# Two-layer graph and state-space kernel: one product for step sizes, gate, B and C, six residual buffers, another order of the scan's small products

## The chip, the cores and the metric

The kernel runs on one core of a Trainium2 chip. A core has five engines that work side by side, each through its own queue in order: TensorE (PE, matrix products, with its weight loads shown apart as PEld), VectorE (DVE), ScalarE (ACT, activations), GpSimd (POOL) and SyncE (SP, which issues transfers). The metric is the device time of the whole kernel in microseconds (us), the median of several runs. All data are float32 unless a line says otherwise.

## What is computed

x is (32, 512, 256), adj is (32, 512, 512) of zeros and ones. Two layers follow each other; each adds a graph part and a feed-forward part to x. Layer 0 is a graph sum with a tropical and a gated classical feed-forward. Layer 1, which the change touches, is an attention over adj (`_L1_gnn_ref`) and a mixer (`_L1_ffn_ref`). The mixer, for each of 32 batches, gathers 512 tokens into 64 slices with softmax weights sw, runs a state-space scan in both directions over the slices, and spreads the result back:

```python
fx = (x @ W_fx.T + b_fx)...                 # 8 heads of 64
sw = softmax((xm @ W_slice.T + b_slice) / temp)
st = einsum('bhnc,bhng->bhgc', fx, sw) / (sw.sum(2) + 1e-5)
ot = _hydra(st, ...)
out = einsum('bhgc,bhng->bhnc', ot, sw) @ out_w.T + out_b

def _hydra(u, ...):
    zxbcdt = u @ in_w.T                     # z 512 | x 512, B 64, C 64 | dt 16
    dt = softplus(concat(dt[:, :, :8], flip(dt[:, :, 8:])) + dt_bias)
    xBC = silu(causal conv of width 3 over xBC + conv_b)
    # h = h * exp(dt * -exp(A_log)) + dt B x ;  y = h C, forward and backward
    y = y_fw + y_bw (each shifted by one) + x * (x @ fcD_w.T + D)
    y = y * silu(z)
    return rms_norm(y) @ out_w.T
```

The kernel does not step through the recurrence: with 64 slices it writes the scan as one product with a decay matrix (the file's gp, segp, decay, mix, yp below).

## The kernel before, in words

`layer1_plain` (L863 on) builds layer 1. Batches are taken in groups of two (GB = 2), so 16 groups. A mixer group is `mixer(g)`: `slices` of each of its two batches, `tokens`, `scan`, and `unslice` of each batch. Two slices of 64 fill the 128 partitions, so a tile in the scan has both batches of its group.

Beside the mixer runs the attention of later batches, `attentions()`: for batch b the products avp and adp (L1258, L1263) are woven with `prepare(b+1)`, which gathers the batch's rows of x, builds its mask, and makes the per-head products hp (L1188). The mixer yields a number at points in its course; the number times PACE is added to a credit, and for each whole unit of credit one step of attention is emitted there. A batch can be prepared only when its rows of x have a buffer: x has AHEAD_X = 2·GB + 1 = 5 buffers (L895), a buffer is free when the batch five before it has been stored by `unslice`. The order of the instructions of each engine is fixed when the kernel is built.

The steps, by tile names:

- `slices`: normalisation of the batch (statistics std, shiftd, x4 by ACT at L1141; the same for the attention with stc, shiftc, hv), lgp (logits, L1344), sw (Exp by ACT L1345, then softmax work on DVE, L1346 to L1351), yTp (L1356) and the turned swT.
- `tokens`: uTp (L1375), rnp (L1381) and on DVE uT.
- `scan`: xp (L1409), which ACT copies to xpad; bcp (L1418), copied to bpad; dtp (L1437 and L1402), from which DVE makes sp, the step sizes (softplus, with ACT's Exp at L1446 and Ln at L1452); zp (L1402), to which ACT applies Silu for z; convolutions with DVE (conv, L1426 to L1428) and Silu with ACT (L1464 for xT, L1471 for B and C, cpad being C with a zero at each end). Then seg (DVE, L1490), gp (L1496), segp (L1500), decay (ACT Exp, L1502), xtp, qp, dq, gm, mix and back (DVE, L1514 to L1519), yp (L1526), y, yTp, oTp (L1544), msp and rms (L1552, L1555), vp (L1566).
- `unslice`: outp (L1576), the addition to the residual rows of x (DVE, L1578), and the store.

psum tiles of this code have four rotating buffers. The weights inT hold the columns in the order z, x, B and C, dt. Each product of float32 shows as two matmuls in the profile.

Of the kernel before, what the change touches and what calls it, by code (L numbers as in the profile page):

```python
# [8 lines left out]
F32 = mybir.dt.float32  # L9
# [4 lines left out]
AF = mybir.ActivationFunctionType  # L14
ALU = mybir.AluOpType
# [4 lines left out]
P = 128  # L20
# [4 lines left out]
LN_EPS = 1e-5  # L25
# [839 lines left out]
def layer1_plain(tc, ident, eps, x2s, ranks, adj, w, out, over, ps):  # L865
# [3 lines left out]
    nc = tc.nc  # L869
    B = adj.shape[0]  # L870
    SEG = B // len(x2s)
    GB = 2
# [19 lines left out]
    AHEAD = 3  # L892
    ATT = 2 * (AHEAD + 2) + AP + 1
    HW = P // AH
    AHEAD_X = 2 * GB + 1  # L895
    PACE = 1.04 * GB * (TURNS + STEPS) / WANTED

    SMALL = 30.0 * 30.0 / D
# [2 lines left out]
    with ExitStack() as ctx:  # L901
# [23 lines left out]
        with tc.tile_pool(name="raw0", bufs=1, side="right") as raw:  # L925
            prod = raw.tile([P, DC, AH, HO], F32, tag="prod", name="prod")
            norm2 = raw.tile([P, DC, 2, AH], F32, tag="norm2", name="norm2")
            for i, name in enumerate(("a_dst", "a_src")):
                dst = wa[:, :, AH * (HO + i) : AH * (HO + i + 1)]
# [30 lines left out]
        bc_w = const("bc_w", [S, 2, KW], w["hy_conv_w"][DI:].rearrange("(c p) k -> p c k", p=S))  # L960
        bc_b = const("bc_b", [S, 2], w["hy_conv_b"][DI:].rearrange("(c p) -> p c", p=S))
        skip = const("skip", [P, H], w["hy_D"].partition_broadcast(P))
        dtb = ctile("dtb", [P, 4, H])
        for i in range(4):
            nc.sync.dma_start(dtb[:, i, :], w["hy_dt_bias"].partition_broadcast(P))
        nega = const("nega", [P, H], w["hy_A_log"].partition_broadcast(P))
        nc.scalar.activation(nega, nega, AF.Exp)
# [20 lines left out]
        wfxT = ctile("wfxT", [P, DC, DI])  # L988
# [3 lines left out]
        inT = ctile("inT", [P, KC, DIN])  # L992
        hoT = ctile("hoT", [P, KC, DI])
        owT = ctile("owT", [P, KC, D])
        fcT = ctile("fcT", [P, KC, H])

        with tc.tile_pool(name="raw", bufs=2, side="right") as raw:
# [4 lines left out]
            for i in range(2):  # L1002
# [4 lines left out]
            nc.sync.dma_start(bs, w["b_slice"].rearrange("(o n) -> o n", o=1))  # L1007


            pieces = [(dst, w[name], r0)  # L1010
                      for dst, name in ((wfxT, "W_fx"), (inT, "hy_in_w"), (hoT, "hy_out_w"), (owT, "out_w"),
                                        (fcT, "hy_fcD_w"))
                      for r0 in range(0, w[name].shape[0], P)]

            def fetch(i):

# [27 lines left out]
            for c in range(DC + 1):  # L1044
                M = P if c < DC else 1
                for i in range(H // KC):

                    half = slice(i * C, (i + 1) * C)
                    px = psum("mm", f"wslp{c}_{i}")
# [3 lines left out]
                    px = px[:M, : KC * G].rearrange("p (k g) -> p k g", k=KC)  # L1053
# [3 lines left out]
                    else:  # L1057
                        dst = bsl[:, i :: H // KC, :]
# [60 lines left out]
        sb = ctx.enter_context(tc.tile_pool(name="s1", bufs=2, reuse_waits="tile"))  # L1119
# [272 lines left out]
        def scan(g, uT):  # L1392


            T = GB * G
# [4 lines left out]
            def tok_matmul(p, c0, n):  # L1400
                for c in range(KC):
                    nc.tensor.matmul(p, uT[:, c, :], inT[:, c, c0 : c0 + n], start=c == 0, stop=c == KC - 1)  # L1402
# [3 lines left out]
            px = psum("any", f"xp{g}")  # L1406
            for k in range(KC):
                for c in range(KC):
                    nc.tensor.matmul(px[:, k * T : (k + 1) * T], inT[:, c, DI + k * P : DI + (k + 1) * P],  # L1409
                                     uT[:, c, :], start=c == 0, stop=c == KC - 1)  # L1410
            xpad = sb.tile([P, KC, GB, LP], F32, tag="xpad", name=f"xpad{g}", bufs=1)
            nc.gpsimd.memset(xpad[:, :, :, : KW - 1], 0.0)
            nc.scalar.copy(xpad[:, :, :, KW - 1 :], px.rearrange("p (k j l) -> p k j l", k=KC, j=GB))
            pb = psum("any", f"bcp{g}")
            for i in range(2):
                c0 = 2 * DI + i * S
                for c in range(KC):
                    nc.tensor.matmul(pb[:S, i * T : (i + 1) * T], inT[:, c, c0 : c0 + S], uT[:, c, :],  # L1418
                                     start=c == 0, stop=c == KC - 1)
            bpad = sb.tile([S, 2, GB, LP], F32, tag="bpad", name=f"bpad{g}", bufs=1)  # L1420
            nc.gpsimd.memset(bpad[:, :, :, : KW - 1], 0.0)
            nc.scalar.copy(bpad[:, :, :, KW - 1 :],
                           pb[:S, : 2 * T].rearrange("p (k j l) -> p k j l", k=2, j=GB))

            def conv(src, wts, dst):
                nc.vector.tensor_scalar_mul(dst, src[:, :, 0:G], wts[:, 0:1])  # L1426
                for q in range(1, KW):
                    nc.vector.scalar_tensor_tensor(dst, src[:, :, q : q + G], wts[:, q : q + 1], dst,  # L1428
                                                   ALU.mult, ALU.add)

            pd = psum("any", f"dtp{g}")
            for j in range(GB):
                for i in range(2):
                    for c in range(KC):
                        nc.tensor.matmul(pd[i * G : (i + 1) * G, j * H : (j + 1) * H],  # L1437
                                         uT[:, c, j * G : (j + 1) * G],
                                         inT[:, c, DT0 + i * H : DT0 + (i + 1) * H],
                                         start=c == 0, stop=c == KC - 1)  # L1440
            tok_matmul(pd[:, 2 * H : 4 * H], DT0, 2 * H)
            sp = sb.tile([P, 5, 4 * H], F32, tag="sp", name=f"sp{g}")
            v, e, u, r, dt = (sp[:, i, :] for i in range(5))
            nc.vector.tensor_add(v, pd[:, : 4 * H], dtb.rearrange("p i h -> p (i h)"))
            nc.vector.scalar_tensor_tensor(e, v, -1.0, v, ALU.mult, ALU.min)
            nc.scalar.activation(e, e, AF.Exp)  # L1446

# [5 lines left out]
            nc.vector.tensor_sub(u, u, e)  # L1453
            nc.vector.scalar_tensor_tensor(dt, v, 0.0, u, ALU.max, ALU.add)

            pz = psum("any", f"zp{g}")
            tok_matmul(pz, 0, DI)
            z = sb.tile([P, DI], F32, tag="z", name=f"z{g}", bufs=1)
            nc.scalar.activation(z, pz, AF.Silu)
            xT = inner(f"xT{g}")  # L1460
            for k in range(KC):
                dst = chunks(xT)[:, k, :]
                conv(xpad[:, k], conv_w[:, k, :], dst.rearrange("p (j l) -> p j l", j=GB))
                nc.scalar.activation(dst, dst, AF.Silu, bias=conv_b[:, k : k + 1])  # L1464
            bcT = sb.tile([S, 2, GB, G], F32, tag="bcT", name=f"bcT{g}", bufs=1)
            cpad = sb.tile([S, GB, G + 2], F32, tag="cpad", name=f"cpad{g}", bufs=1)
            nc.gpsimd.memset(cpad[:, :, 0 : G + 2 : G + 1], 0.0)
            for i in range(2):
                conv(bpad[:, i], bc_w[:, i, :], bcT[:, i])
                dst = bcT[:, 0] if i == 0 else cpad[:, :, 1 : G + 1]  # L1470
                nc.scalar.activation(dst, bcT[:, i], AF.Silu, bias=bc_b[:, i : i + 1])  # L1471

            la = sb.tile([P, GB, H], F32, tag="la", name=f"la{g}")
# [15 lines left out]
            yield 7  # L1491

            pg = psum("any", f"gp{g}")
            for j in range(GB):
                for i in range(2):
                    nc.tensor.matmul(pg[j * G : (j + 1) * G, i * G : (i + 1) * G], bcT[:, 0, j, :],  # L1496
                                     cpad[:, j, 2 * i : 2 * i + G], start=True, stop=True)
            pl = psum("any", f"segp{g}")
            for j in range(GB):
                nc.tensor.matmul(pl[j * G : (j + 1) * G, :], seg_l, seg[j], start=True, stop=True)  # L1500
            decay = inner(f"decay{g}")
            nc.scalar.activation(decay, pl, AF.Exp)  # L1502
# [17 lines left out]

            yield 7
            py = psum("any", f"yp{g}")
            for j in range(GB):
                half = slice(j * G, (j + 1) * G)
                for h in range(H):
                    nc.tensor.matmul(py[half, h * C : (h + 1) * C], heads(mix)[half, h, :],  # L1526
                                     heads(xk)[half, h, :], start=True, stop=True)
            y = inner(f"y{g}")
# [3 lines left out]
            ms = sb.tile([P, 1], F32, tag="ms", name=f"ms{g}")  # L1532
# [13 lines left out]
            oT = inner(f"oT{g}")  # L1546
            nc.scalar.copy(oT, po)

            pm = psum("any", f"msp{g}")
            for j in range(GB):  # L1550
                for i in range(P // C):
                    nc.tensor.matmul(pm[i * G : (i + 1) * G, j : j + 1], ident[:, j * G : (j + 1) * G], ms,  # L1552
                                     start=True, stop=True)
            rms = sb.tile([P, GB], F32, tag="rms", name=f"rms{g}")
            nc.vector.tensor_scalar(rms, pm[:, :GB], 1.0 / DI, LN_EPS, ALU.mult, ALU.add)  # L1555
            nc.gpsimd.tensor_tensor(rms, rms, eps[:, 1:2].to_broadcast([P, GB]), ALU.pow)
            yield 2

# [690 lines left out]
```

## Time and profile before

| what | us |
|---|---|
| time, median of 3 runs | 4320.41 (4319.69 to 4325.92) |
| the profiled execution's own time | 4319.15 |
| its span | 4317.4 |
| TensorE busy in the span | 3852.3 |
| VectorE busy | 3233.1 |
| ScalarE busy | 2290.3 |
| mixer groups' first xp product, from first to last | 2490.99 to 4249.27 |
| per group, mean of 15 steps | 117.2 |

The kernel's first 2330 us or so are layer 0. The groups of layer 1 have a step of 115 to 120 us, and 103 at the end, where no attention is left to weave in. Group 14 has little of it and group 15 none. Busy time adds all instructions of an engine; the time that an engine waits is shown with what ended the wait. A name such as `xp<-inT,uT` is output tile, then operands; the number after x counts instructions. The granted clock of TensorE is in tenths or as a share, 1.00 being full.

### The profile page before, as it was taken

How to read it: one execution, taken by the hardware profiler on the slowest of the kernel's cores; microseconds unless marked ns; L12 is line 12 of the kernel's file. 1: busy time of each engine (PE TensorE's matmuls, PEld its weight loads, DVE VectorE, ACT ScalarE, POOL GpSimd, SP SyncE). 2: the span in 40 equal slices, each digit the busy share in tenths (PEclk: the TensorE clock that was granted, in tenths of full speed). 3: DMA queues.
4: the chain of work that ended last, by engine and by line, in shares of the span. 5: the costliest groups of instructions: out<-in, count | busy, mean ns of one | idle time of the engine just before them, and what ended most of it. 6: DMA issues, size and time to landing. Idle time of an engine off the chain costs nothing.

```text
span 4317.4 us, 57903 instructions
## 1 busy us (share of the span) xinstructions
PE 3852.3 (89%) x20311; PEld 2446.7 (57%) x20311; DVE 3233.1 (75%) x7008; ACT 2290.3 (53%) x4756; POOL 1540.2 (36%) x1940
## 2 busy tenths in 40 slices
PE   5567998899999999889998899999999999999997
PEld 4454565566655665555555355565555555565555
DVE  6668877888788977877775777767777777778763
ACT  3344655556655656556664455545554455555432
POOL 2355643664435644354332222222222222222210
PEclk8678999999999999999999999999999999999998
DMA  4557654665546654386542322222222232222210
GB/s 130 161 160 228 191 162 133 192 214 168 149 127 218 197 165 136 109 279 192 153 128 69 78 67 71 79 62 67 74 69 69 76 79 76 75 69 74 62 30 16
DMA packets 260811, 524.16 MB, mean 121 GB/s; under 512 B 39800, under 2 KB 131588, under 8 KB 260509
## 3 DMA queue, kind: packets, MB, share of 16 engines
q0 software_dynamic: 124800, 366.28, 29.5%
q1 hardware_dynamic: 135708, 154.08, 11.4%
q8 instruction: 162, 2.65, 0.3%
q14 instruction: 141, 1.15, 0.1%
HBM read 463.11 MB, written 57.17 MB: 121 GB/s over the span
## 4 chain that ended last, share of the span: by engine, by line
PE 35%; DVE 26%; DMA 10%; issue 9%; POOL 8%; ACT 5%; SPq 0%; POOLq 0%; DVEq 0%; ACTq 0%
PE clsp L623 5%; DVE att L1221 4%; PE gatep L623 4%; PE po L652 3%; PE avp L1258 3%; DVE acc L637 3%; DMA rows<-table,xs 2%; PE yTp L1356 2%; DVE best L599 2%; DMA best<-table,xs 2%; DVE sw L1351 2%; DMA rows<-table,tops 2%; DVE sst L1349 2%; DVE sw L1346 2%; PE oTp L1544 1%
## 5 line engine op out<-in xcount | busy, mean ns | idle before, releaser
L623 PE MATMUL clsp<-xnT,wc 128*128 128x512 f32 x1024 | 522.4, 629 | 47.2 <-ACT cls L625 40.3
L623 PE MATMUL gatep<-xnT,wg 128*128 128x512 f32 x1024 | 496.8, 604 | 9.4 <-ACT gate L625 7.4
L652 PE MATMUL po<-wd,acc 128*128 128x256 f32 x2048 | 451.7, 380 | 5.2 <-DVE acc L641 4.3
L652 PEld LDWEIGHTS po<-wd,acc 128*128 128x128 f32 x2048 | 386.8, 190 | 70.7 <-issue 9.1
L1221 DVE SCALAR_TENSOR_TENSOR att<-own,other,mask 128x512 f32<-128x512 f32 x512 | 365.7, 743 | 78.5 <-DMA own<-ownd 78.5
L599 DVE SCALAR_TENSOR_TENSOR best<-rows,xs,best 128x1024 f32<-128x1024 f32 x212 | 271.0, 1280 | 132.6 <-ACT best L593 74.9
L637 DVE SCALAR_TENSOR_TENSOR acc<-past,fld,acc 128x512 f32<-128x512 f32 x448 | 332.1, 744 | 32.5 <-ACT past L636 24.3
L623 PEld LDWEIGHTS gatep<-xnT,wg 128*128 128x128 f32 x1024 | 196.1, 196 | 249.9 <-issue 198.4
L632 ACT ACTIVATE acc<-tz,fld 128x512 f32<-128x512 f32 x256 | 199.0, 777 | 260.1 <-PE tz L630 235.2
L636 ACT ACTIVATE past<-tz,fld 128x512 f32<-128x512 f32 x448 | 291.3, 693 | 73.3 <-DVE acc L637 72.7
L596 POOL DMA_INDIRECT rows<-table,xs x212 | 252.9, 1193 | 188.6 <-DVE best L599 124.8
L623 PEld LDWEIGHTS clsp<-xnT,wc 128*128 128x128 f32 x1024 | 183.7, 200 | 184.6 <-issue 113.3
L435 PE MATMUL pm<-h,adj 128*128 128x258 f32 (+1 forms) x1024 | 182.3, 325 | 98.5 <-DVE keep L428 35.7
L1258 PE MATMUL avp<-att,hv 128*32 128x512 f32 x2048 | 254.9, 603 | 13.9 <-DVE att L1221 13.8
L625 ACT ACTIVATE gate<-gatep,fld 128x512 f32<-128x512 f32 x256 | 175.5, 685 | 158.3 <-PE gatep L623 129.2
L1344 PE MATMUL lgp<-wsl,x4T 128*128 128x512 f32 x512 | 243.0, 613 | 16.6 <-ACT sw L1345 7.2
L1356 PE MATMUL yTp<-sw,x 128*128 128x512 f32 x512 | 237.8, 602 | 18.9 <-DVE sw L1351 18.2
L554 POOL DMA_INDIRECT xs<-rows_of,order x128 | 155.0, 1211 | 266.8 <-DVE acc L637 104.3
L1162 POOL DMA_INDIRECT x<-x2s,ranks x128 | 136.5, 1066 | 297.7 <-DVE att L1221 133.3
L1309 POOL TENSOR_TENSOR mu<-mu,eps 128x16 f32<-128x16 f32 x32 | 111.2, 3475 | 348.1 <-DVE mu L1308 347.9
L1576 PE MATMUL outp<-v,swT 128*128 128x256 f32 x1024 | 227.6, 381 | 0.0
L435 PEld LDWEIGHTS pm<-h,adj 128*128 128x128 f32 x1024 | 152.5, 214 | 123.9 <-issue 73.0
(590 smaller groups left out, 8643.8 us busy)
## 6 DMA issues: line engine op xcount, KB each, us to landing
adj<-in_adj POOLq DMA_DIRECT2D x128, 256.0 KB, 5.6
ai<-in_adj SPq DMA_DIRECT2D x128, 256.0 KB, 2.8
x<-added POOLq DMA_DIRECT2D x64, 512.0 KB, 5.2
own<-ownd SPq DMA_DIRECT2D x128, 256.0 KB, 3.6
rows_of<-keep SPq DMA_DIRECT2D x32, 550.0 KB, 4.3
x<-in_x SPq DMA_DIRECT2D x32, 512.0 KB, 6.6
xs<-bd POOLq DMA_DIRECT2D x32, 512.0 KB, 5.7
x2s<-xs SPq DMA_DIRECT2D x32, 512.0 KB, 3.0
```

Of the source, the lines that this page charges most:

```text
L435: nc.tensor.matmul(pm[:, : c1 - c0], a[:, i, t * P : (t + 1) * P], h[:, i, c0:c1], start=i + c0 == 0, stop=i + 1 == NT and c0 > 0)
L596: nc.gpsimd.indirect_dma_start(out=row, out_offset=None, in_=table, in_offset=bass.IndirectOffsetOnAxis(ap=idxs[:, k : k + 1].bitcast(U32) ...
L599: nc.vector.scalar_tensor_tensor(m, row, vals[:, k : k + 1], m, ALU.add, ALU.max)
L623: nc.tensor.matmul(pf, wf[:, c, f * P : (f + 1) * P], xnT[:, c, :], start=c == 0, stop=c == DC - 1)
L636: nc.scalar.activation(r, z, AF.Relu, bias=fld[:, f, AT + b : AT + b + 1])
L637: nc.vector.scalar_tensor_tensor(y, r, fld[:, f, CH + b : CH + b + 1], y, ALU.mult, ALU.add)
L652: nc.tensor.matmul(po[:, i, :], acc[f][:, t * P : (t + 1) * P], wd[:, f, :], start=f == 0, stop=f == FC - 1)
L1221: nc.vector.scalar_tensor_tensor(e, own[h], other[:, j, h : h + 1], mask[:, j, :], ALU.max, ALU.mult)
L1258: nc.tensor.matmul(pv[p][k * HW : (k + 1) * HW, :], hv[:, j, h, e : e + HW], weighed[b, h, j], **ends)
L1344: nc.tensor.matmul(pf, xnT[:, c, t * P : (t + 1) * P], wsl[:, c, :], start=c == 0, stop=c == DC - 1)
L1356: nc.tensor.matmul(py, xn[:, t, c * P : (c + 1) * P], sw[:, t, :], start=t == 0, stop=t == NT - 1)
L1576: nc.tensor.matmul(po[:, :D], swT[:, k, t * P : (t + 1) * P], v[:, k, :], start=k == 0, stop=k == KC - 1)
```

## The change

The columns of inT are stored in the order dt (16), z (512), x (512), B and C (128). B and C are one product over 128 output rows, into the first 128 columns of the bcp bank; dt and the first half of z are one product of 272 columns into the rest of that bank; the second half of z has its own bank with 256 columns. The products that wrote dt half by half in the partitions of each direction are gone: DVE instead adds the bias with one instruction over the 16 columns and four over halves of the partitions. B and C are convolved as one tile of 128 partitions. z and the convolution and Silu of B and C are written ahead of those of x. The mean square of rms is read on DVE by four small instructions and no longer copied by PE (msp). The loops of gp and yp have the halves of the group innermost, segp runs its halves in reverse. sp and la have one buffer, x has six.

```diff
-    AHEAD_X = 2 * GB + 1
+    AHEAD_X = 2 * GB + 2
...
-        dtb = ctile("dtb", [P, 4, H])
-        for i in range(4):
+        dtb = ctile("dtb", [P, 2, H])
+        for i in range(2):
...
-            pb = psum("any", f"bcp{g}")
-            for i in range(2):
-                c0 = 2 * DI + i * S
-                for c in range(KC):
-                    nc.tensor.matmul(pb[:S, i * T : (i + 1) * T], inT[:, c, c0 : c0 + S], uT[:, c, :],
-                                     start=c == 0, stop=c == KC - 1)
-            bpad = sb.tile([S, 2, GB, LP], F32, tag="bpad", name=f"bpad{g}", bufs=1)
...
+            pb, pz = psum("any", f"bcp{g}"), psum("any", f"zp{g}")
+            for c in range(KC):
+                nc.tensor.matmul(pb[:, :T], inT[:, c, DIN - P :], uT[:, c, :], start=c == 0, stop=c == KC - 1)
+            first = 2 * H + DI // 2
+            tok_matmul(pb[:, T : T + first], 0, first)
+            tok_matmul(pz[:, : DI // 2], first, DI // 2)
+            bpad = sb.tile([P, GB, LP], F32, tag="bpad", name=f"bpad{g}", bufs=1)
+            nc.gpsimd.memset(bpad[:, :, : KW - 1], 0.0)
+            nc.scalar.copy(bpad[:, :, KW - 1 :], pb[:, :T].rearrange("p (j l) -> p j l", j=GB))
...
-            pd = psum("any", f"dtp{g}")
-            for j in range(GB):
-                for i in range(2):
-                    for c in range(KC):
-                        nc.tensor.matmul(pd[i * G : (i + 1) * G, j * H : (j + 1) * H],
-                                         uT[:, c, j * G : (j + 1) * G],
-                                         inT[:, c, DT0 + i * H : DT0 + (i + 1) * H],
-                                         start=c == 0, stop=c == KC - 1)
-            tok_matmul(pd[:, 2 * H : 4 * H], DT0, 2 * H)
-            sp = sb.tile([P, 5, 4 * H], F32, tag="sp", name=f"sp{g}")
+            pd = pb[:, T : T + 2 * H]
+            sp = sb.tile([P, 5, 4 * H], F32, tag="sp", name=f"sp{g}", bufs=1)
             v, e, u, r, dt = (sp[:, i, :] for i in range(5))
-            nc.vector.tensor_add(v, pd[:, : 4 * H], dtb.rearrange("p i h -> p (i h)"))
+            nc.vector.tensor_add(v[:, 2 * H :], pd, dtb.rearrange("p i h -> p (i h)"))
+            for i in range(2):
+                for j in range(GB):
+                    half = slice(j * G, (j + 1) * G)
+                    nc.vector.tensor_add(v[i * G : (i + 1) * G, j * H : (j + 1) * H],
+                                         pd[half, i * H : (i + 1) * H], dtb[half, 0, :])
...
-            pz = psum("any", f"zp{g}")
-            tok_matmul(pz, 0, DI)
             z = sb.tile([P, DI], F32, tag="z", name=f"z{g}", bufs=1)
-            nc.scalar.activation(z, pz, AF.Silu)
+            nc.scalar.activation(z[:, : DI // 2], pb[:, T + 2 * H : T + first], AF.Silu)
+            nc.scalar.activation(z[:, DI // 2 :], pz[:, : DI // 2], AF.Silu)
+            bcT = sb.tile([P, GB, G], F32, tag="bcT", name=f"bcT{g}", bufs=1)
+            cpad = sb.tile([S, GB, G + 2], F32, tag="cpad", name=f"cpad{g}", bufs=1)
+            nc.gpsimd.memset(cpad[:, :, 0 : G + 2 : G + 1], 0.0)
+            conv(bpad, bc_w, bcT)
+            for half, dst in ((slice(0, S), bcT[:S]), (slice(S, P), cpad[:, :, 1 : G + 1])):
+                nc.scalar.activation(dst, bcT[half], AF.Silu, bias=bc_b[half])
...
-            for j in range(GB):
-                for i in range(2):
-                    nc.tensor.matmul(pg[j * G : (j + 1) * G, i * G : (i + 1) * G], bcT[:, 0, j, :],
+            for i in range(2):
+                for j in range(GB):
+                    nc.tensor.matmul(pg[j * G : (j + 1) * G, i * G : (i + 1) * G], bcT[:S, j, :],
                                      cpad[:, j, 2 * i : 2 * i + G], start=True, stop=True)
             pl = psum("any", f"segp{g}")
-            for j in range(GB):
+            for j in reversed(range(GB)):
                 nc.tensor.matmul(pl[j * G : (j + 1) * G, :], seg_l, seg[j], start=True, stop=True)
...
-            for j in range(GB):
-                half = slice(j * G, (j + 1) * G)
-                for h in range(H):
+            for h in range(H):
+                for j in range(GB):
+                    half = slice(j * G, (j + 1) * G)
                     nc.tensor.matmul(py[half, h * C : (h + 1) * C], heads(mix)[half, h, :],
                                      heads(xk)[half, h, :], start=True, stop=True)
...
-            pm = psum("any", f"msp{g}")
+            rms = sb.tile([P, GB], F32, tag="rms", name=f"rms{g}")
             for j in range(GB):
                 for i in range(P // C):
-                    nc.tensor.matmul(pm[i * G : (i + 1) * G, j : j + 1], ident[:, j * G : (j + 1) * G], ms,
-                                     start=True, stop=True)
-            rms = sb.tile([P, GB], F32, tag="rms", name=f"rms{g}")
-            nc.vector.tensor_scalar(rms, pm[:, :GB], 1.0 / DI, LN_EPS, ALU.mult, ALU.add)
+                    nc.vector.tensor_scalar(rms[i * G : (i + 1) * G, j : j + 1], ms[j * G : (j + 1) * G], 1.0 / DI, LN_EPS,
+                                            ALU.mult, ALU.add)
```

The preparation of the weights follows (the pieces of in_w are copied to the new columns, conv weights and biases of B and C lie in 128 partitions).

More of the change, by code (lines that the diff above doesn't have):

```diff
@@ L959, in layer1_plain @@
         conv_b = const("conv_b", [P, KC], w["hy_conv_b"][:DI].rearrange("(c p) -> p c", p=P))
-        bc_w = const("bc_w", [S, 2, KW], w["hy_conv_w"][DI:].rearrange("(c p) k -> p c k", p=S))
-        bc_b = const("bc_b", [S, 2], w["hy_conv_b"][DI:].rearrange("(c p) -> p c", p=S))
+        bc_w = const("bc_w", [P, KW], w["hy_conv_w"][DI:])
+        bc_b = const("bc_b", [P, 1], w["hy_conv_b"][DI:].rearrange("(p o) -> p o", o=1))
         skip = const("skip", [P, H], w["hy_D"].partition_broadcast(P))
-        dtb = ctile("dtb", [P, 4, H])
-        for i in range(4):
+        dtb = ctile("dtb", [P, 2, H])
+        for i in range(2):
             nc.sync.dma_start(dtb[:, i, :], w["hy_dt_bias"].partition_broadcast(P))
@@ L1007, in layer1_plain @@
             nc.sync.dma_start(bs, w["b_slice"].rearrange("(o n) -> o n", o=1))
[L1010 to L1013, printed above, removed]
+            pieces = [(dst, src, r0)
+                      for dst, src in ((wfxT, w["W_fx"]), (inT[:, :, 2 * H :], w["hy_in_w"][:DT0]),
+                                       (inT[:, :, : 2 * H], w["hy_in_w"][DT0:]), (hoT, w["hy_out_w"]),
+                                       (owT, w["out_w"]), (fcT, w["hy_fcD_w"]))
+                      for r0 in range(0, src.shape[0], P)]
             def fetch(i):
@@ L1408, in scan @@
                 for c in range(KC):
-                    nc.tensor.matmul(px[:, k * T : (k + 1) * T], inT[:, c, DI + k * P : DI + (k + 1) * P],
-                                     uT[:, c, :], start=c == 0, stop=c == KC - 1)
+                    x0 = 2 * H + DI + k * P
+                    nc.tensor.matmul(px[:, k * T : (k + 1) * T], inT[:, c, x0 : x0 + P], uT[:, c, :],
+                                     start=c == 0, stop=c == KC - 1)
             xpad = sb.tile([P, KC, GB, LP], F32, tag="xpad", name=f"xpad{g}", bufs=1)
@@ L1413, in scan @@
             nc.scalar.copy(xpad[:, :, :, KW - 1 :], px.rearrange("p (k j l) -> p k j l", k=KC, j=GB))
-            pb = psum("any", f"bcp{g}")
-            for i in range(2):
-                c0 = 2 * DI + i * S
-                for c in range(KC):
-                    nc.tensor.matmul(pb[:S, i * T : (i + 1) * T], inT[:, c, c0 : c0 + S], uT[:, c, :],
-                                     start=c == 0, stop=c == KC - 1)
-            bpad = sb.tile([S, 2, GB, LP], F32, tag="bpad", name=f"bpad{g}", bufs=1)
-            nc.gpsimd.memset(bpad[:, :, :, : KW - 1], 0.0)
-            nc.scalar.copy(bpad[:, :, :, KW - 1 :],
-                           pb[:S, : 2 * T].rearrange("p (k j l) -> p k j l", k=2, j=GB))
+            pb, pz = psum("any", f"bcp{g}"), psum("any", f"zp{g}")
[7 more added lines that the diff above has]
+            nc.scalar.copy(bpad[:, :, KW - 1 :], pb[:, :T].rearrange("p (j l) -> p j l", j=GB))
             def conv(src, wts, dst):
@@ L1464, in scan @@
                 nc.scalar.activation(dst, dst, AF.Silu, bias=conv_b[:, k : k + 1])
-            bcT = sb.tile([S, 2, GB, G], F32, tag="bcT", name=f"bcT{g}", bufs=1)
-            cpad = sb.tile([S, GB, G + 2], F32, tag="cpad", name=f"cpad{g}", bufs=1)
-            nc.gpsimd.memset(cpad[:, :, 0 : G + 2 : G + 1], 0.0)
-            for i in range(2):
[L1469 to L1475, printed above, removed]
+            la = sb.tile([P, GB, H], F32, tag="la", name=f"la{g}", bufs=1)
             nc.vector.tensor_mul(la, dt[:, : GB * H].rearrange("p (j h) -> p j h", j=GB),
@@ L1493, in scan @@
             pg = psum("any", f"gp{g}")
-            for j in range(GB):
-                for i in range(2):
-                    nc.tensor.matmul(pg[j * G : (j + 1) * G, i * G : (i + 1) * G], bcT[:, 0, j, :],
+            for i in range(2):
+                for j in range(GB):
+                    nc.tensor.matmul(pg[j * G : (j + 1) * G, i * G : (i + 1) * G], bcT[:S, j, :],
                                      cpad[:, j, 2 * i : 2 * i + G], start=True, stop=True)
             pl = psum("any", f"segp{g}")
-            for j in range(GB):
+            for j in reversed(range(GB)):
                 nc.tensor.matmul(pl[j * G : (j + 1) * G, :], seg_l, seg[j], start=True, stop=True)
```

## The prediction

> **What bounds the kernel now.** I read the busy totals first, then the same totals by stretches of 500 us, then the waits of TensorE (PE) between 2500 and 4100 us, then the scan of one mixer group (group 5) instruction by instruction.
>
> ```profile
> PE 3852.3 (89%) x20311; PEld 2446.7 (57%) x20311; DVE 3233.1 (75%) x7008; ACT 2290.3 (53%) x4756; POOL 1540.2 (36%) x1940
> ...
> 2500.00:3000.00 500.00, 473.54 (x3225) 287.64 (x3224) 365.17 (x835) 264.63 (x684) 126.45 (x119) 1.00 0.27 70
> 3000.00:3500.00 500.00, 478.50 (x3247) 296.30 (x3246) 369.40 (x830) 253.71 (x652) 128.27 (x118) 1.00 0.28 74
> ```
> Columns of the stretches: length, busy time of PE, its weight loads, DVE, ACT, POOL, then granted clock. Layer 1 fills the time from about 2330 us on; its 16 groups start their scans (first xp product) at 2490.99, 2610.68 ... 4249.27, 118 us apart. In that steady part PE is busy 95 to 96% of the time; about 5 us of a group's 118 are open. So PE is the bound over the whole, and the question is whether that holds in the one stretch that the change shortens.
>
> ```profile
> PE yTp L1356 <- DVE sw L1351: 15.2, 19, 1.0
> PE oTp L1544 <- ACT yT L1538: 12.1, 14, 1.1
> PE maskp L1092 <- ACT sw L1345: 7.4, 6, 1.3
> PE lgp L1344 <- ACT sw L1345: 7.2, 7, 1.6
> PE lgp L1344 <- DVE x L1578: 6.7, 7, 2.0
> ...
> DVE stc L1134 <- DMA x<-x2s,ranks: 42.8, 41, 2.7
> ```
> Total us, times, longest. PE's largest waits lie in slices (lgp, yTp, with sw), few in the scan: there only oTp and yp.
>
> Group 5's scan, the chain of waits between 3088 and 3117 us, and ACT's timeline of the same time:
>
> ```profile
> 3088.58 3.77 PE xp L1409 x32
> 3092.35 1.89 PE bcp L1418 x16
> 3094.24 1.20 PE dtp L1437 x32
> 3095.44 0.99 PE dtp L1402 x8
> 3096.43 3.53 PE zp L1402 x8
> ...
> 3105.92 0.39 PE gp L1496 x8
> 3106.31 1.35 PE segp L1500 x4
> ...
> 3113.80 1.83 PE yp L1526 x32
> ```
> ```profile
> 3096.38 1.28 ACT L1446 ACT_TABLE_LOAD   x1
> 3097.67 0.23 ACT L1446 ACTIVATE sp<-sp 128x32 f32<-128x32 f32 x1
> ...
> 3102.20 0.23 ACT L1452 ACTIVATE sp<-sp 128x32 f32<-128x32 f32 x1
> 3102.45 1.28 ACT L1464 ACT_TABLE_LOAD   x1
> ...
> 3104.34 0.39 ACT L1471 ACTIVATE cpad<-bcT,bc_b 64x128 f32<-64x128 f32 x1
> ```
> The chain through the scan is all PE, with attention's products (avp, adp, hp) as filler between zp and gp. But ACT ends cpad at 3104.73 and PE reaches gp at 3105.85: the chain Exp, Ln, Silu with its table loads is only 1.1 us behind PE. That margin decides what PE's saving is worth.
>
> **What the Trainium skill says.** "TensorE: Matmul & The Clock Gate", Part 3, says that small products in different row or column groups of the array run at the same time. The trace agrees: vp (halves alternating) takes 3.67 us for 32 products of 256 columns, outp on the whole array takes 7.17 for 32 of the same width. Part 1 of that page says that PE's clock is halved after an idle window of about 3.4 us. Here 2.01 us of idle before lgp was followed by 3.40 us for four products that take 1.98 elsewhere, so less seems enough. "ScalarE: Activation LUTs", What ACT_TABLE_LOAD costs, gives 1283 ns and a drain, some 2.66 us in all; here the next activation starts as the 1.28 us end (3096.38, then 3097.67), so I use 1.29.
>
> **The change, part by part.**
> 1. *Projections.* Removed per group: bcp 1.89 + dtp 1.20 + 0.99 + zp 3.53 = 7.61 us of PE. Added: 8 products over 128 columns at 0.118 (xp's 3.77/32) = 0.94; 8 over 272 columns, priced by hp's 264 columns at 0.245 = 1.96; 8 over 256 columns at outp's 0.219 (7.17/32 below) = 1.75. Sum 4.65, so −2.96. The four msp products go too (8 in the records), −0.33.
> 2. *Order of yp and gp.* With the halves alternating, yp's 1.83 becomes about 1.15: 32 × 36 ns, what rnp shows for 32 small products over 64 columns. Bounds 0.9 and 1.83. I take −0.68, and gp −0.1. Reversing segp moves nothing by itself: 1.35 either way; it now starts on the last of the two seg tiles.
> 3. *PE in sum:* −2.96 − 0.33 − 0.68 − 0.1 = −4.07 per group, 65 us over 16. That is an upper limit, not yet a gain.
> 4. *VectorE.* The step sizes come in one add over 16 columns and four small half-partition adds (about 0.11 apart), then four rms instead of one: +8 at 0.11; bcT's convolution loses 3 of 6 instructions at 0.27: about +0.1 to +0.3. sp and la get one buffer in place of two; their next write is 118 us after the last, long after mix has read dt, so that costs nothing.
> 5. *Where ACT and DVE stand.* Both engines are served in order, and the built order differs. DVE now runs all xT convolutions (3.2 us from 3094.6) and the 1.14 us add into x before the step sizes, so e is ready near 3099.6, not 3096.9. ACT then runs table, Exp (near 3100.8), one square of attention's edges 0.6, table, B's Silu, table, Ln (near 3104.7, not 3102.20), table, cpad (done near 3106.5, not 3104.73). The number of table loads stays six. DVE then puts shiftd ahead of seg, and shiftd waits for POOL's rsd, 1.4 us behind mvd: seg's second half is done near 3108.3, not 3106.54.
> 6. *What that does to PE.* With 2.96 saved and one avp/adp pair (1.85) moved ahead of gp, PE reaches gp near 3104.7 to 3105.5, waits about 1 us for cpad and about 1.45 for seg, and ends segp near 3109.1. Queued behind it are xtp, qp (to 3110.7) and decay; ACT's three normalising activations and a table load stand before decay, which ends near 3110.6. DVE's dq waits for qp, then five instructions of 0.62 each (mix, back, y, mix, mix by decay) end near 3114.1. yp follows, 1.15, to 3115.3 against 3115.63 before. So some 0.2 to 0.3 us of the 4.07 remain: the rest has turned into waits on ACT's tables and DVE. Bounds: −3 (if ACT gets ahead) and +2.5 (a slow clock after the waits). I take −0.2 × 16 = −3.
> 7. *Sixth buffer.* Before, the gather into x of batch 2g+5 waits for the store of batch 2g, which has just been unsliced, and DVE stands at its first statistics (stc). For group 4 at 3024 us: 2.39 + 1.81 + 0.57 = 4.8 us, and the last outp add stands behind it. PE's lgp waited 2.01 us for that add, and its first products were then 1.4 us slow. ACT's four hv activations (2.08 us) come ahead of sw too, and PE waits for that (1.26 and 0.37 in the sw rows). Summed over groups 0 to 13, PE's idle time from vp to the next uTp is some 52 us and slow products 2.3: 3.9 per group. With six buffers the stc wait leaves the place before the last outp add in groups 2, 5, 8 and 11, stays in most others with another batch, and hv leaves the place before sw. What is late next is DVE's own softmax (yTp waits for sw, 15.2 us already). So not all 3.9 comes: bounds 0 and 3.9, I take 1.7 × 14 = −24. SP's stores and POOL's gathers keep their number; SP has two dtb loads fewer, once. POOL's rsd now stands ahead of the memset of cpad, which had kept it waiting for gp (69.8 us, 12 times in cpad's row): that helps shiftd, and is in step 5's time.
> 8. *Tail.* Groups 14 and 15 have no filler. In group 15 PE stood 4.36 us before gp and 3.48 before yp: all of PE's saving there waits for ACT. Shorter projections start ACT's chain some 1 us sooner; in group 14 attention's last vector work stands between the mix steps: 0 ± 3.
>
> Sum: −3 − 24 = −27 from the profiled execution's own 4319.15 us (span 4317.4 and 1.75 around it), so 4292. That execution stands 1.3 us below the median of 4320.41; predicted 4293.
>
> **Rivals.**
> - *PE stays the bound in the scan.* For it: the chain is all PE and 95% busy; the walk of step 5 has an error of 1 us per link, and fillers could be drawn into the waits. Against: the filler's order is fixed at build, and ACT's margin is 1.1 us. All of 65 and 24: 4319 − 89, or 4231 beside the median; half of the 65: 4264.
> - *No change.* Step 6 comes out at nothing and the gather's wait only moves to another batch. For it: in ten of 14 groups a wait of the same kind stays. 4316 to 4320.
> - *Slower.* One mechanism: in each scan ACT's B Silu between Exp and Ln costs a table load, and shiftd stands before seg. It decides from yp's end 1.5 us later than before in each group (24/16), which is 1.7 beyond step 6. At +3 (2 us of error in the walk, 1.2 of slow clock such as lgp's, less the 0.2): 16 × 3 − 24 = +24 on 4319.15, so 4343, or 4344 beside the median. For it: PE waits of 2 us have slowed the clock before. Against: it needs every group.
>
> **How the numbers follow.** A measurement here tells 0.2% (8.6 us) from no change. Chances: the forecast's case (4262 to 4311) 0.47; PE-bound (below 4262) 0.20; no change 0.13; slower 0.20. Faster 0.67, same 0.13, slower 0.20. The range, 4252 to 4330, takes in most of the first three and leaves out 0.1 at either end; the likeliest case's own is 4270 to 4311.
>
> **What would show it.** In the changed profile: zp and bcp with 272 and 256 columns near 4.65 us; yp near 1.15 (if 1.83, step 2 fails); PE waiting at gp for ACT cpad and at segp for DVE seg (if neither shows, the first rival holds); Ln near 12 us after xp's end, not 9.9; stc's wait for the gather clearly under 42.8 and the rows of lgp behind the outp add gone. If yp's wait for mix grows beyond 3 us a group, the slower rival is true.

## The result and the profile after

| what | before | after |
|---|---|---|
| time, median of 6 runs each, side by side, us | 4325.39 (4319.69 to 4336.23) | 4355.46 (4342.23 to 4365.51) |
| span of the profiled execution, us | 4317.4 | 4352.2 |
| TensorE busy in it, us | 3852.3 | 3822.0 |

The changed kernel is slower: the ratio is 1.0068, with a 95% interval from 1.0047 to 1.0089. In the first part of the page after, PE's matmul records fell by 768 (20311 before), but its busy time only by 30 us:

```profile
PE 3822.0 (88%) x19543; PEld 2424.9 (56%) x19543; DVE 3232.5 (74%) x7072; ACT 2292.7 (53%) x4771; POOL 1566.3 (36%) x1940
```

The stretches of 500 us in the steady part of layer 1, after:

```profile
2500.00:3000.00 500.00, 461.90 (x3019) 279.29 (x3012) 368.79 (x853) 254.84 (x654) 131.15 (x115) 0.98 0.26 69
3000.00:3500.00 500.00, 457.44 (x2985) 276.67 (x2984) 360.37 (x839) 262.70 (x682) 129.68 (x118) 0.98 0.26 71
```

PE is busy 91 to 92% here, 95 to 96% before, and its granted clock is 0.98 in place of 1.00. PE has become a little freer and a little slower. The waits of PE and one of DVE between 2500 and 4130 us say where it stands now:

```profile
PE yTp L1358 <- DVE sw L1353: 23.4, 33, 1.3
PE gp L1493 <- ACT cpad L1463: 17.3, 14, 3.6
PE segp L1497 <- DVE seg L1487: 16.7, 13, 1.5
...
PE lgp L1346 <- DVE x L1573: 11.2, 8, 1.7
PE lgp L1346 <- DVE mask L1095: 11.2, 6, 1.9
...
PE yp L1523 <- DVE mix L1516: 3.8, 10, 1.1
...
DVE stc L1136 <- DMA x<-x2s,ranks: 33.1, 33, 2.9
```

Three rows of the same stretch before:

```profile
PE yTp L1356 <- DVE sw L1351: 16.0, 20, 1.0
...
PE yp L1526 <- DVE mix L1519: 3.5, 5, 1.4
...
PE lgp L1344 <- DVE mask L1093: 1.1, 6, 0.2
```

Two rows are new, gp behind cpad and segp behind seg: 34 us. The two rows of lgp and maskp behind ACT's sw, 14.6 us before, are gone, but yTp behind sw, lgp behind the outp add (6.7 before) and lgp behind the mask copies have grown.

From the starts of PE's products I cut each group into stages and summed them over groups 0 to 13 (the first stage, from uTp to the scan's first product, belongs to groups 1 to 14):

| us, 14 groups | uTp to scan | scan to gp | gp to yp | yp to oTp | oTp to vp | vp to next uTp | sum |
|---|---|---|---|---|---|---|---|
| before | 105.1 | 245.4 | 108.7 | 76.0 | 63.2 | 1056.6 | 1655.0 |
| after | 105.2 | 254.8 | 126.8 | 70.4 | 63.2 | 1056.6 | 1677.0 |

The scan lost 22 us, and the part from vp to the next uTp neither gained nor lost. The remaining 13 us lie before the first group: its first xp product starts at 2504.07 instead of 2490.99. Of that, 1.6 us are there already 560 us earlier, at one of layer 0's last classical products; from there to the first xp product it takes 558.1 us before and 569.6 after (+11.5). The last two groups take the same time (−0.2). 1.6 + 11.5 + 22.0 − 0.2 is 34.9, and the spans differ by 34.8.

**Inside one scan.** The chain of waits of group 5 after, from 3107 to 3126 us, with pieces left out where the dots stand:

```profile
3107.12 3.36 POOL mu L1311
3110.50 1.23 DVE av L1314
...
3114.61 1.14 DVE x L1315
3115.75 0.08 DVE sp L1438
...
3122.90 0.20 POOL rsd L30
...
3123.18 1.02 POOL rsd L31
3124.22 0.16 DVE shiftd L1141
3124.39 1.22 DVE seg L1487 x2
...
3125.74 1.08 PE segp L1497 x4
```

Before, PE carried this chain from xp to yp. Now PE is not on it until segp: it runs through DVE's queue, with attention's av and x in front of the step sizes and POOL's rsd and shiftd in front of seg. ACT in the same group:

```profile
3118.17 0.23 ACT L1445 ACTIVATE sp<-sp 128x32 f32<-128x32 f32 x1
...
3119.03 1.28 ACT L1463 ACT_TABLE_LOAD   x1
3120.32 0.40 ACT L1463 ACTIVATE bcT<-bcT,bc_b 64x128 f32<-64x128 f32 x1
3120.74 1.28 ACT L1451 ACT_TABLE_LOAD   x1
3122.03 0.23 ACT L1451 ACTIVATE sp<-sp 128x32 f32<-128x32 f32 x1
3122.28 1.28 ACT L1463 ACT_TABLE_LOAD   x1
3123.58 0.40 ACT L1463 ACTIVATE cpad<-bcT,bc_b 64x128 f32<-64x128 f32 x1
```

Exp, then B's Silu between two table loads, then Ln, then a third load and cpad. PE's timeline of the same group shows what it waits for (the bracket: idle time and releaser):

```profile
3124.03 0.45 PE L1493 MATMUL gp<-cpad,bcT 64*64 64x64 f32 x8 [1.03 <-ACT cpad L1463]
3125.74 1.08 PE L1497 MATMUL segp<-seg,seg_l 128*64 128x512 f32 x4 [1.26 <-DVE seg L1487]
...
3131.68 1.15 PE L1523 MATMUL yp<-xk,mix 64*64 64x64 f32 x32 [0.27 <-DVE mix L1516]
```

The two waits have different last links: gp waits for the end of ACT's chain, and segp for seg, which stands on DVE behind shiftd.

**The clock.** Groups with the same order of instructions on PE differ between gp and yp. Here each row is one group's stretch from gp to yp, after (groups 5, 6, 7, 8 and 9); the column after POOL's is the granted clock. Groups 5, 7 and 8 have one order; groups 6 and 9 have another, with mask products (maskp) in it:

```profile
3124.03:3131.68 7.65, 5.88 (x41) 4.14 (x41) 4.83 (x10) 6.80 (x19) 1.17 (x3) 1.00 0.01 2
3242.57:3253.05 10.48, 9.11 (x40) 5.77 (x40) 5.67 (x12) 6.36 (x12) 0.69 (x2) 0.59 0.00 0
3365.85:3375.00 9.15, 7.39 (x40) 4.85 (x41) 4.83 (x10) 6.91 (x19) 1.16 (x3) 0.81 0.00 1
3486.36:3494.01 7.65, 5.88 (x40) 4.14 (x41) 4.83 (x10) 6.80 (x19) 1.17 (x3) 1.00 0.01 3
3603.60:3613.31 9.71, 8.34 (x41) 5.76 (x41) 5.67 (x12) 6.36 (x12) 0.70 (x2) 0.65 0.00 0
```

Where the clock is 1.00, groups 5 and 8 take 7.65 us; before, group 5 took 7.88, with two of the attention's products more in the stretch. In 8 of the first 14 groups the clock is between 0.59 and 0.87 and the stretch 1 to 3 us longer than before (more in group 0, which has other fillers: 12.96 against 8.97). Groups 0 and 3 wait otherwise than group 5. In the other 12, PE waits 1.03 to 1.08 us before gp and 1.24 to 1.29 before segp; six of them have a clock of 0.59 to 0.81, and six, of both orders, keep 1.00.

### The profile page after: what moved, and what is told of

It is laid out like the page before. It is cut to its first block, busy times and chain, and to the rows that moved or that the text cites. A ratio compares the mean times of both kernels' runs of the same rounds, so it can differ in the third digit from the quotient of the medians.

```text
span 4352.2 us, 56431 instructions
## 1 busy us (share of the span) xinstructions
PE 3822.0 (88%) x19543; PEld 2424.9 (56%) x19543; DVE 3232.5 (74%) x7072; ACT 2292.7 (53%) x4771; POOL 1566.3 (36%) x1940
## 3 DMA queue, kind: packets, MB, share of 16 engines
q1 hardware_dynamic: 135420, 154.07, 11.2%
q14 instruction: 140, 1.15, 0.1%
## 4 chain that ended last, share of the span: by engine, by line
DVE 23%; PE 15%; ACT 6%; POOL 5%; DMA 5%; issue 4%; SPq 0%; DVEq 0%; POOLq 0%; ACTq 0%
DVE att L1223 5%; PE yTp L1358 2%; PE clsp L623 2%; PE gatep L623 2%; DVE sw L1353 2%; POOL mu L1311 2%; DVE sst L1351 2%; PE oTp L1541 2%; DVE sw L1348 1%; DVE mask L1095 1%; PE po L652 1%; DMA own<-ownd 1%; PE outp L1571 1%; POOL x L1164 1%; DMA rows<-table,tops 1%
## 5 line engine op out<-in xcount | busy, mean ns | idle before, releaser
L623 PE MATMUL clsp<-xnT,wc 128*128 128x512 f32 x1024 | 524.1, 630 | 33.1 <-ACT cls L625 27.9
L652 PEld LDWEIGHTS po<-wd,acc 128*128 128x128 f32 x2048 | 388.4, 191 | 71.5 <-issue 9.3
L1164 POOL DMA_INDIRECT x<-x2s,ranks x128 | 161.9, 1265 | 374.6 <-DVE att L1223 161.3
L1260 PE MATMUL avp<-att,hv 128*32 128x512 f32 x2048 | 273.8, 603 | 23.3 <-DVE att L1223 23.2
L1346 PE MATMUL lgp<-wsl,x4T 128*128 128x512 f32 x512 | 239.6, 607 | 24.1 <-DVE x L1573 11.2
```

Source lines behind the costliest of these rows:

```text
L623: nc.tensor.matmul(pf, wf[:, c, f * P : (f + 1) * P], xnT[:, c, :], start=c == 0, stop=c == DC - 1)
L652: nc.tensor.matmul(po[:, i, :], acc[f][:, t * P : (t + 1) * P], wd[:, f, :], start=f == 0, stop=f == FC - 1)
L1260: nc.tensor.matmul(pv[p][k * HW : (k + 1) * HW, :], hv[:, j, h, e : e + HW], weighed[b, h, j], **ends)
L1346: nc.tensor.matmul(pf, xnT[:, c, t * P : (t + 1) * P], wsl[:, c, :], start=c == 0, stop=c == DC - 1)
```

## The experiments

The medians of the kernel before were 4332.33 beside the first four runs, 4332.63 beside the next four and 4322.72 beside the last, so ratios are compared, not times. "Passage" is the stretch from layer 0's late classical product to the first product of the first scan.

| run | ratio to before | 95% interval | passage, us | uTp to yp | yp to oTp | vp to next uTp |
|---|---|---|---|---|---|---|
| before | 1 | | 558.1 | 459.2 | 76.0 | 1056.6 |
| after | 1.0068 | 1.0047 to 1.0089 | 569.6 | 486.8 | 70.4 | 1056.6 |
| bcw_two_loads | 1.0056 | 1.0042 to 1.0070 | 561.0 | 494.1 | 71.5 | 1058.8 |
| five_buffers | 1.0062 | 1.0045 to 1.0078 | 574.8 | 493.6 | 66.9 | 1050.8 |
| steps_first | 0.9920 | 0.9903 to 0.9937 | 572.9 | 431.9 | 67.8 | 1055.5 |
| halves_only | 0.9945 | 0.9929 to 0.9960 | 556.6 | 459.3 | 66.4 | 1049.6 |
| gp_four_times | 1.0064 | 1.0044 to 1.0083 | 574.2 | 488.4 | 68.6 | 1056.1 |
| two_bias_loads | 1.0021 | 1.0013 to 1.0029 | 571.0 | 459.2 | 76.0 | 1055.7 |
| steps_first_two_loads | 0.9911 | 0.9896 to 0.9925 | 557.6 | 431.9 | 67.7 | 1055.8 |
| steps_first_two_loads_five | 0.9891 | 0.9874 to 0.9907 | 558.7 | 428.7 | 67.5 | 1051.7 |
| both_gaps_filled | 1.0052 | 1.0035 to 1.0069 | 569.2 | 477.9 | 69.9 | 1053.3 |

(The stages are of one profiled execution each, summed over 14 groups. Where xp is the last of the projections, the passage is taken to the first projection, 4.6 us before xp.)

### Step sizes first: is the late chain the scan's loss?

```diff
-            px = psum("any", f"xp{g}")
...
             pb, pz = psum("any", f"bcp{g}"), psum("any", f"zp{g}")
+            first = 2 * H + DI // 2
+            tok_matmul(pb[:, T : T + first], 0, first)
             for c in range(KC):
                 nc.tensor.matmul(pb[:, :T], inT[:, c, DIN - P :], uT[:, c, :], start=c == 0, stop=c == KC - 1)
-            first = 2 * H + DI // 2
-            tok_matmul(pb[:, T : T + first], 0, first)
             tok_matmul(pz[:, : DI // 2], first, DI // 2)
...
             nc.vector.scalar_tensor_tensor(dt, v, 0.0, u, ALU.max, ALU.add)
+            px = psum("any", f"xp{g}")
...
```

> The changed kernel, with the same products in another order: step sizes and gate first, then B and C, then the gate's second half, then xp; the step sizes' vector work is written ahead of x's. Theory 1 (the loss in the scan is the late chain e, Exp, B's Silu with its table load, Ln, cpad, seg, in front of gp and segp): Ln is done some 5 us earlier after the first product, gp and segp no longer wait, from the first product to oTp about 29 us instead of 33.0 in the mean (31.4 before), so 16 x 3.5 to 4 = 55 to 65 us under the changed kernel: 4290 to 4300. Rival (the scan's loss is PE's slow clock and contention whatever the order, or PE waits for DVE's work in total): within 15 us of 4355.

Measured: 0.9920, and 4297.39 us. From uTp to yp 431.9 us against 486.8 of the changed kernel, 55 us less over 14 groups with the same work. The waits of PE in the same stretch of layer 1 in this run, two of its rows:

```profile
PE segp L1497 <- DVE seg L1487: 3.4, 3, 2.0
...
PE gp L1493 <- ACT cpad L1463: 2.0, 2, 1.8
```

From 34.0 to 5.4 us. In group 5, ACT ends cpad 0.33 us before PE comes to gp:

```profile
3104.73 0.23 ACT L1430 ACTIVATE sp<-sp 128x32 f32<-128x32 f32 x1
...
3107.16 0.40 ACT L1463 ACTIVATE cpad<-bcT,bc_b 64x128 f32<-64x128 f32 x1
```

On PE, a filler stands between gp and segp:

```profile
3106.92 1.04 PE L1265 MATMUL adp<-att,hv 128*32 128x512 f32 x8
3107.89 0.45 PE L1493 MATMUL gp<-cpad,bcT 64*64 64x64 f32 x8
3108.27 1.93 PE L1260 MATMUL avp<-att,hv 128*32 128x512 f32 x16
3110.01 1.02 PE L1265 MATMUL adp<-att,hv 128*32 128x512 f32 x2
3110.96 1.08 PE L1497 MATMUL segp<-seg,seg_l 128*64 128x512 f32 x4
```

So the merged products do save time when the chain behind them is not late: against the kernel before, the scan and the products ahead of it are 27 us shorter (459.2 to 431.9), and yp to oTp 8. The run does not tell apart B's Silu between Exp and Ln, the step sizes behind x's work on DVE, and shiftd before seg: it moves all of them. Its trace says something about the first: ACT still loads six tables in the scan of group 5, and a Silu (of z) still stands between Exp and Ln, yet Ln starts 10.4 us after the scan's first product instead of 16.5, as DVE begins with the step sizes 3.0 us after that product instead of 10.1. So the table load between Exp and Ln isn't what this run took away. The clock is part of the gain: it is 1.00 from gp to yp in groups 1 to 13 of this run.

### The two idle times and the clock

```diff
             pg = psum("any", f"gp{g}")
-            for i in range(2):
+            for i in (0, 1) * 4:
```

> The changed kernel with each product of gp done four times over into the same place (the result is the same, PE has some 1.16 us more to do in each group, beginning when cpad is there and ending before seg is). Theory (of the changed kernel's loss in the scan, the part between gp and yp, 126.8 us over 14 groups against 108.7, is a halved clock after the two short idle times in front of gp and segp; with PE busy over most of the second, the clock holds): gp to yp back to the 7.63 of the undisturbed groups in nearly all groups, a sum near 110, so about 15 us under the changed kernel in spite of more work, 4335 to 4345. Rival (PE is late anyway, more work costs its time): 16 x 1.16 = 18 us over it, near 4374. Third possibility (the wait for seg covers it and the clock is not the matter): no change, 4352 to 4360.

Measured: 1.0064 and a sum of 128.5 from gp to yp: the expected 110 did not come. The undisturbed groups now take 7.97 (not 7.63), and 6 of 14 are still far above that (8 in the changed kernel). Only the second of the two gaps had been filled, and that in part (0.55 us of 1.25 are left), and the run decided nothing. The next one fills both:

```diff
             pg = psum("any", f"gp{g}")
+            for _ in range(8):
+                nc.tensor.matmul(pg[:G, 2 * G : 4 * G], bcT[:S, 0, :], bcT[:S].rearrange("p j l -> p (j l)"),
+                                 start=True, stop=True)
-            for i in range(2):
+            for i in (0, 1) * 4:
```

> The changed kernel with both idle times in front of gp and segp filled by useless products: eight of B with B (8 x 0.12 to 0.24 us, into columns that nothing reads) before gp, and gp's own done four times as in the run gp_four_times; one adp unit of 0.86 us falls behind qp. Theory (idle time in front of gp and segp halves PE's clock in some groups): granted clock between gp and yp 1.00 in all of the groups 1 to 13 (it was under 0.9 in 8 of the first 14), gp to yp 7.7 to 8.5 in each, the sum over 14 groups 110 to 118 instead of 126.8, time 8 to 15 us under the changed kernel's 4355 to 4360 in spite of some 2.5 us more of PE work per group. Rival 1 (PE work is the bound): 16 x 2.5 = 40 us slower. Rival 2 (clock drops are set elsewhere): as many groups with a clock under 0.9 as before.

The stretches from xp to yp of this run, groups 5, 6 and 9:

```profile
3094.22:3120.68 26.46, 25.65 (x216) 16.60 (x212) 20.77 (x59) 19.26 (x40) 5.78 (x7) 1.00 0.18 41
3214.05:3241.14 27.09, 24.88 (x212) 15.74 (x208) 21.26 (x59) 19.04 (x39) 5.78 (x7) 1.00 0.17 40
...
3570.06:3597.15 27.09, 24.88 (x212) 15.74 (x209) 21.26 (x59) 19.04 (x39) 5.80 (x7) 1.00 0.18 40
```

The clock is 1.00 in each of groups 0 to 13, and groups 6 and 9 take 27.09 where they took 29.03 and 28.27. The built order changed too: products of the attention that stood before gp now lie between the useless products and gp, so the gaps are filled by both. From xp to yp the 14 groups need 372.7 us instead of 381.6, though PE has more to do. The ratio, 1.0052, lies below the changed kernel's 1.0068, by less than the intervals tell apart; the clock in the trace is the evidence, not the time. It shows that idle time in front of gp and segp costs clock, and that more PE work there costs little: 0.3 us in group 5, whose clock was 1.00 without it (26.46 against 26.15 from xp to yp).

### The halves alone

```diff
-            for j in range(GB):
-                half = slice(j * G, (j + 1) * G)
-                for h in range(H):
+            for h in range(H):
+                for j in range(GB):
+                    half = slice(j * G, (j + 1) * G)
                     nc.tensor.matmul(py[half, h * C : (h + 1) * C], heads(mix)[half, h, :],
...
```

The same for gp, and rms on DVE in place of msp, as in the change; all else is the kernel before.

> The kernel before with two of the edits alone: yp and gp with the halves alternating, and rms read on DVE instead of through msp. PE saves 0.68 + 0.1 + 0.33 = 1.1 us per group. Theory 1 (PE's saving counts where no other engine is late; yp is on the path to oTp, gp and msp are not): yp to oTp shorter by 0.5 to 0.7, so 8 to 12 us under the kernel before. Rival (PE is the bound everywhere): 18 us under it. Third possibility (filler work only moves): within 4 us.

Measured: 0.9945, about 24 us of the 4332 beside it, more than either theory had. yp to oTp is 9.6 us shorter over 14 groups, as expected, and vp to the next uTp 7.0, which was not. These small edits alone bring some two thirds of what the whole set brings with step sizes first (0.55% against 0.80%). The saved 18 us of PE lie within the interval (17 to 31 us), so the rival fits best. In the part from vp on, one wait has gone from the trace: lgp behind the outp add, 6.7 us before, a wait that step 7 of the prediction laid to the want of a sixth buffer. How these edits removed it was not followed up.

### The sixth buffer

```diff
-    AHEAD_X = 2 * GB + 2
+    AHEAD_X = 2 * GB + 1
```

> The changed kernel with five buffers of x instead of six. Theory 1 (the sixth buffer gained nothing: the time from vp to the next uTp summed over 14 groups was 1056.6 us before and after, since waits on the softmax chain of DVE replaced those on the gather): 4350 to 4362, vp to uTp again within 10 us of 1056. Rival A (it did gain the predicted 24 us, and the other edits cost as much more): slower by 15 to 25 us, near 4375. Rival B (it costs, by moving attention work into the scan): faster by over 10 us.

Measured: 1.0062, not to be told from the changed kernel's 1.0068; vp to uTp 1050.8, within the 10 us of Theory 1. Four rows of the waits of PE and one of DVE in this run show the exchange:

```profile
PE yTp L1358 <- DVE sw L1353: 15.9, 20, 1.0
...
PE lgp L1346 <- ACT sw L1347: 6.8, 5, 1.6
...
PE lgp L1346 <- DVE mask L1095: 1.3, 6, 0.2
...
PE lgp L1346 <- DVE x L1573: 0.7, 2, 0.5
...
DVE stc L1136 <- DMA x<-x2s,ranks: 34.1, 36, 3.1
```

With five buffers, ACT's hv activations stand before sw again (6.8 here and 6.9 for maskp); with six they do not, but yTp then waits 23.4 for DVE's softmax instead of 15.9, and lgp 11.2 for the mask copies and 11.2 for the outp add instead of 1.3 and 0.7. The wait for the gather is the same, 34.1 against 33.1. In the traces the sixth buffer costs some us: with the new order of gp and yp, the stretch from vp to uTp takes 1049.6 to 1051.7 us in the three kernels with five buffers and 1053.3 to 1058.8 in the six with six. Six buffers with the kernel before were not tried.

### The passage

```diff
-        bc_w = const("bc_w", [P, KW], w["hy_conv_w"][DI:])
+        bc_w = ctile("bc_w", [P, KW])
+        for i in range(2):
+            nc.sync.dma_start(bc_w[i * S : (i + 1) * S], w["hy_conv_w"][DI + i * S : DI + (i + 1) * S])
```

> The changed kernel, with the convolution weights of B and C loaded by two transfers of 64 rows instead of one of 128: nothing else differs in layer 1's groups, but the order built for the passage from layer 0 to layer 1 falls back almost to that of the kernel before (setup work such as Exp of A_log stands where it stood). Theory 1 (the 13 us by which the first group started later are an accident of that order): first xp product near 2492 instead of 2504, time about 10 to 13 us under the changed kernel's 4355, so 4343. Rival (the late start is noise of layer 0, or belongs to the sixth buffer): no change, 4350 to 4360.

The passage took 561.0 us, about as with the order of before, but the ratio (1.0056) moved by 0.0012 only, which the intervals tell neither from nothing nor from the 10 us expected. In the traces the groups' sum was 10.6 us above the changed kernel's, 7.3 of it from gp to yp (134.1 against 126.8), where the clock drops in 10 groups instead of 8. So I turned it round and gave the kernel before the passage of the changed one:

```diff
-        for i in range(4):
+        for i in range(2):
             nc.sync.dma_start(dtb[:, i, :], w["hy_dt_bias"].partition_broadcast(P))
+        nc.vector.tensor_copy(dtb[:, 2:], dtb[:, :2])
```

> The kernel before with one edit in its set-up: the step sizes' bias is loaded by two transfers instead of four, and copied to the other half on DVE. Nothing in the groups differs, but the built order of the passage from layer 0 to layer 1 becomes that of the changed kernel. Theory (the order of the passage costs about 14 us: from the same late classical product of layer 0 to the first xp product 558.1, 561.0 and 556.6 us in three kernels with the one order, 569.6, 574.8 and about 573 in three with the other): that stretch near 571, time 10 to 14 us over the kernel before. Rival (the stretches differ by chance): within 4 us of the kernel before.

Measured: 1.0021 (1.0013 to 1.0029), 9 us, with a passage of 571.0 and groups like those of before. Over all kernels, the passage took 556.6 to 561.0 us with the one order and 569.2 to 574.8 with the other. What PE waits for there, in the changed kernel's timeline:

```profile
1996.36 0.40 PE L1094 MATMUL maskp<-identb,a 128*128 128x128 bf16 x4 [1.19 <-ACT a L1103]
1996.97 0.40 PE L1094 MATMUL maskp<-identb,a 128*128 128x128 bf16 x4 [0.21 <-ACT a L1103]
2003.31 0.61 PE L1094 MATMUL maskp<-identb,a 128*128 128x128 bf16 x4 [5.94 <-ACT a L1103]
2004.92 0.61 PE L1094 MATMUL maskp<-identb,a 128*128 128x128 bf16 x4 [1.00 <-ACT a L1103]
```

The four products of layer 1's first mask follow each other at once, and PE's queue stands behind them for 8.3 us; the longest wait, 5.94, is for an activation that itself waits 3.92 us for the transfer of its rows of adj. Before, gate and class products of layer 0 lie between the four, and only 1.3 us are lost to them. That is 7 of the 11.5 us; the rest was not followed up.

### The best of them

> Step sizes first, together with the two loads of B's and C's weights that give the passage the order of before. If both effects add: some 11 to 14 us under the 4297 of step sizes first alone, 4283 to 4287; relative to the kernel before 0.989. If the passage's order is no matter: 4292 to 4300.

> The same with five buffers of x. Theory (the sixth buffer is worth nothing): within 5 us of the run with six. Rival (now that the scan is shorter, the gather's wait counts): 10 to 20 us slower with five.

Both are step sizes first with the two loads of bc_w, the second with five buffers. Measured: 0.9911 and 0.9891 (4295.39 and 4284.39 us). The passage fell to 557.6 as expected, but the time of the first moved by 0.0009 only, less than the intervals can show. With five buffers it is 11 us faster at the median, while the intervals overlap; in the traces vp to uTp is 4 us shorter and the scan 3. The sixth buffer is worth nothing here either, and by the traces it costs. The last version beats both kernels, the one before by 1.1% (0.9 to 1.3).

## Why the prediction was wrong

Between the forecast's −27 us and the 34.8 by which the spans differ lie 62: 25 of the scan (22 lost where step 6 had 3 gained), 24 of the sixth buffer (step 7), 11.5 of the passage and 1.6 ahead of it.

**Steps 1 to 3, the work saved: right.** The three remaining small projections of group 5 run from 3109.2 to 3113.7 us, 4.5 against 4.65; yp takes the predicted 1.15. gp did not shrink (0.45 against 0.46). In the last version above (0.9891), where the clock is 1.00 from gp to yp in groups 0 to 13, PE is busy for 3792.8 us, 59.5 less than before, of the 65 of step 3.

**Step 4, DVE: right in sign.** Four half-partition adds take 0.69 us together, 0.17 each where I had 0.11.

**Step 5, the chain: right.** Counted from the first xp product, Exp was to start after 12.3 us, Ln after 16.2, cpad to end after 18.0 and seg after 19.8. In group 5 it is 12.6, 16.5, 18.4 and 20.1.

**Step 6, the scan's sum: wrong, by a value taken at the wrong end of its bounds.** yp was to start 25.7 us after the first xp product, and starts after 26.1 where the clock holds. From xp to oTp an undisturbed group takes 30.89 us against 30.42 before (group 5: 18.50 + 7.65 + 4.74 against 17.34 + 7.88 + 5.20): +0.5, not −0.2. Of that, 0.2 are there at yp's end, where the step stopped counting (27.30 against 27.12), and 0.3 come between there and oTp. If group 5 stands for all, that accounts for 7 of the 22 us, and by this reckoning the other 15 are clock; filling the gaps took 9 of them back in spite of the added work. I had put a slow clock after the waits into the upper bound of +2.5, with the example of lgp at hand, and then took −0.2 for all groups; measured is +1.6 in the mean (22/14). "TensorE: Matmul & The Clock Gate", Part 1 (What's actually happening), says that the window which sets the clock runs freely and doesn't start with the kernel's work. That would explain why groups with one order fare differently; no run here shows the window itself.

**Step 7, the sixth buffer: wrong.** It had −24 us and gave 0. The waits that it was to remove did go (lgp and maskp behind ACT's sw, 14.6 us), and I named DVE's softmax as what is late next, but kept 1.7 of 3.9 us in each group. Nothing of it was left: yTp behind sw rose from 16.0 to 23.4 in this stretch, lgp behind the outp add from 6.7 to 11.2, and lgp behind the mask copies from 1.1 to 11.2. The 0 has two parts: with five buffers the changed kernel takes 5.8 us less from vp to uTp than before, and the sixth buffer puts them back. The sign that I had named for it, a shorter wait for the gather, came without it: 42.8 before, 34.1 with five buffers, 33.1 with six. The sum of idle times in a stretch was no measure of what one of its causes is worth; that several chains end there at about the same time would explain it, and is argued, not shown.

**What no step had: the passage.** Two transfers fewer were booked as "once", at nothing. They are done at a place where the built order of two layers is woven together, and the order fell differently: 11.5 us in the trace, 9 us by the run with that edit (and a copy on DVE) alone.

**The slower rival** had the place and the late chain in the scan, and its 4344 was closer than the forecast, in part by luck: it had 48 us of loss in the scan where 22 were measured, a gain of 24 that didn't come, and nothing for the passage. Its sign did not show: yp's wait for mix was to grow beyond 3 us a group and is 3.8 us in all (3.5 before). It set its point of decision from the 24 us that weren't there; without them, any loss in the scan makes the kernel slower.

## What to carry to other kernels

Saving work on the busiest engine pays only as far as the chain that feeds its next product is early; move that chain's first product forward together with the saving (1.1% faster instead of 0.7% slower here, with the passage's old order and one buffer fewer). A buffer more is to be tried alone: here it cost what the other edits had gained in the stretch that it was to shorten. Where engine queues are woven at build time, compare the order far away from the edit too: two small loads fewer in the set-up cost 9 us. And where a margin of idle time is created on PE, price its clock, not only the wait.

## What the runs showed of the hardware

After two idle times of PE of about 1.05 and 1.26 us, with 0.45 us of work between, its granted clock was 0.59 to 0.81 in the mean from gp to yp in 6 of 12 groups, while the other six, with the same instructions, kept 1.00. With useless products and moved fillers in the gaps, all 14 groups had 1.00. And the 32 products of 64 by 64 of yp take 1.90 us in the timeline when they stay in one half of the partitions for 16 in a row, and 1.15 when the halves alternate:

```profile
3113.73 1.90 PE L1526 MATMUL yp<-xk,mix 64*64 64x64 f32 x32
```
